# Two-layer graph network on one core: moving the value weights' sums and tile 1's attention in the opening pairs

## The chip, the cores and the metric

The kernel runs on one core of a Trainium2 chip, as a single program. The metric is its time on the device in microseconds; lower is better. A core has five engines that run side by side [...]: TensorE (PE in the profile; its weight loads are listed as PEld), VectorE (DVE), ScalarE (ACT), GpSimd (POOL), and SyncE (SP), which here issues most of the transfers between the device's memory (DRAM) and the on-chip memory (SBUF). Each engine takes its own instructions strictly in order. Results of TensorE land in PSUM banks and are read from there by VectorE or ScalarE. All data are fp32.

## The reference: what is computed

There are 128 graphs of 64 nodes with 768 features. Layer 0 is a graph attention layer with 12 heads of 64 features and a gate, layer 1 an attention layer with 6 heads of 128 features; each is added to its input and normalized:

```python
# layer 0
h = einsum('bnd,ade->bane', x, W)                  # 12 heads
th = tanh(h)
attn = th @ w_src + swap(th @ w_dst)               # one number for each pair of nodes
attn = where(attn >= 0, attn, 0.2 * attn)
attn = softmax(where(~adj, -999.0, attn))
f = elu(attn @ h + b)
gate = sigmoid(x @ H_w.T + H_b)
x = layernorm(x + gate * f + (1 - gate) * x)
# layer 1
q, k, v = x @ Wq + bq, x @ Wk + bk, x @ Wv + bv    # 6 heads
probs = softmax(q @ k.T / sqrt(128) + where(adj, 0, -9e15))
x = layernorm(x + (probs @ v) @ Wf + bf)
```

The layer-1 values v = x @ Wv are computed already in the first phase, pair by pair, as soon as a pair's layer-0 rows are known. They are the only part of layer 1 that the change touches.

## The kernel before

**Tiles and pairs.** The 8192 rows are 64 tiles of 128 rows (two graphs each). Two tiles make a pair p (tiles 2p and 2p+1), so layer 0 has 32 pairs. For a pair, h of all 12 heads and the gate's input are one matrix product: 256 rows by 768, times 768 by 1536. The kernel does it with a scheme that needs 15 block products, called a0 to a14, in place of 18 (class Fifteen). Each takes its own left operand, a block of x or a sum of blocks (made by GpSimd in x_sums, L886), and its own right operand, one of 15 weight blocks. Only 9 of these are loaded as they are; the other weights are sums of them, which VectorE makes at the start (made, L871, 17 steps of 128x1024). The first pair, p = 0, cannot wait for the sums and is computed plainly with the raw blocks (class Plain, 18 products, L987). One product is four matmuls of 128x512.

**Banks.** Products accumulate along five paths (the first number in PRODUCTS), each in a PSUM bank of its own: a0, a3, a6, a9, a11, a13 share one, a8, a10, a12, a14 another, a5 and a7 a third, a2 and a4 a fourth. Between two products of a path the bank is read: its content is added to, or copied into, the tile's buffer hg. This read is the product's way out. The first one into a place is a copy on ScalarE (L968, or L970 with its sign turned), a later one an addition on VectorE (L966). The next product of the path may start only when the way out of the one before has been done.

**Attention of layer 0, for each tile t.** The steps, with the names that the order uses: tanh (function products: tanh on ScalarE, L1019; products with the attention vectors, one half on VectorE, L1020, then the other on GpSimd, L1021), terms (a reduction on VectorE, L1029, and a transpose), send and fetch (the terms to DRAM and back, spread over all partitions), bias (GpSimd, L1052), hx (a copy of the other half of h), logits and leaky (6 ScalarE instructions each, L1072), masked (VectorE: mask L1086 and maximum L1092), exps (12 ScalarE instructions, L1101), probs (transposes on TensorE and copies back), attend (TensorE), feat (VectorE, and an exponential on ScalarE), elu, gated, stats (VectorE), pow (GpSimd), norm (ScalarE), byf (transposes of the result on TensorE, L1113, copied back by ScalarE). Beside them go gbias (GpSimd, L1232), gtanh (ScalarE, L1237 and L1238), resid (GpSimd, L1164), mask (ScalarE turns adj into the mask, L1226), and inputs and plus (loads of x).

**Values.** For each pair the products v1 to v7 (class Job, L349) compute x1 @ Wv with 7 block products in place of 8. They need sums of Wv's four blocks B11, B21, B22, T3: T1 = T3 - B11, T2 = B22 - T1, T4 = B21 - T2, T3 = B22 - T3 (function weight_sums, L295 to L298, one VectorE operation of 128x1152 each), and sums of the rows x1, sum0 to sum3 (L319 to L322). The four blocks are loaded by four transfers of 576 KB on SP's queue (L290).

**The order.** It is written out by hand. EARLY and TURN list the products of all pairs, interleaved; the position of a product in this list is its item. After the product of item i TensorE's instructions are followed, in program order, by the way out of the product of item i - 1, and then by all steps that the plan has put on item i, sorted by their position. The tables NEW_EARLY, OLD_EARLY and SUMS_EARLY (one dict each for p = 0 to 3) give these positions: in OLD_EARLY relative to EARLY_OLD[p] (22 for the first pair) or, for xT and adj, to the start of the next pair; in NEW_EARLY relative to the last of the products that the step needs. Each engine then takes its own instructions in exactly this order. Pair 0 has items 0 to 17, pair 1 items 18 to 32, pair 2 and the values of pair 0 items 33 to 54.

Of the kernel before, what the change touches and what calls it, by code (L numbers as in the profile page):

```python
# [133 lines left out]
EARLY = (  # L134
    "a0 a1 a2 a3 a4 a5 a6 a7 a8 a9 a10 a11 a12 a13 a14 a15 a16 a17".split(),
    "a0 a5 a1 a3 a8 a7 a6 a10 a2 a9 a12 a4 a11 a14 a13".split(),
    "a0 a5 a3 a1 a8 a7 a6 u1 u2 u6 u5 u7 a2 a10 a9 a4 u4 a12 a11 a14 a13 u3".split(),
    "a0 a5 a3 a1 u1 u2 u6 a8 u5 u7 a7 u4 u3 a6 a10 a2 a12 a9 a14 a11 a4 a13 v1 v2".split(),
)
EARLY_OLD = (22, 41, 60)  # L140

# [13 lines left out]
SUMS_LAST = dict(next6=0.4, next9=6.4, next2=0.6, next3=5, next0=15.7, next5=0.1, next8=11.3, own10=1.2, own12=7.8,  # L155
    own13=10.6)
OLD_LAST = dict(probs1=2.1, gtanh1=0.8, resid1=5.8, attend1=5, feat1=5.5, elu1=7, gated1=7.4, stats1=9.3,
    pow1=10.8, norm1=11.6, byf1=13.3, spill1=14.5, logits0=3, leaky0=3.4, masked0=4.4, exps0=5,
    gtanh0=8, resid0=9.7, probs0=8.8, attend0=10.5, feat0=11.8, elu0=12.4, gated0=12.8, stats0=14.5,
    pow0=14.6, norm0=15.6, byf0=16.5, spill0=22.4, sum0=16.5, sum1=17.2, sum2=18.5, sum3=24.4,  # L160
    spillT=24.8, spillV=11, mask=5.1, adj=-1.3, xT=3.4, inputs1=5.9, inputs0=18.5, plus1=13.6,
    plus0=18.9)
OLD_EARLY = [
    dict(probs1=3.1, gtanh1=-2, resid1=-1.5, attend1=3.8, feat1=5, elu1=5.5, gated1=6.1, stats1=7.3,
        pow1=8, norm1=9.8, byf1=10, spill1=13.3, logits0=3.5, leaky0=4.8, masked0=5.2, exps0=7.2,
        gtanh0=3.5, resid0=4.8, probs0=9.8, attend0=10.5, feat0=12, elu0=12.2, gated0=12.3, stats0=14.2,
        pow0=15, norm0=15.7, byf0=17.8, spill0=18.8, sum0=10.2, sum1=18, sum2=19.9, sum3=24.9,
        spillT=21.4, spillV=18.5, mask=7.7, adj=3.9, xT=-5.3, inputs1=6.2, inputs0=17.3, plus1=11.2,
        plus0=18.8),
    dict(probs1=-3.8, gtanh1=1.8, resid1=2.5, attend1=3.3, feat1=4.7, elu1=5.6, gated1=5.8, stats1=6.3,  # L170
        pow1=7, norm1=8, byf1=10, spill1=12.7, logits0=2, leaky0=4, masked0=4.8, exps0=6.8, gtanh0=3.7,
        resid0=6, probs0=8, attend0=9.2, feat0=9.5, elu0=12, gated0=12.4, stats0=13, pow0=14, norm0=16,
        byf0=17, spill0=22, sum0=14.1, sum1=18, sum2=21.5, sum3=24.2, spillT=23, spillV=15.2, mask=5.7,
        adj=4.9, xT=-0.8, inputs1=10.6, inputs0=13.7, plus1=18.5, plus0=14.2),
    dict(probs1=-0.5, gtanh1=1.9, resid1=3.8, attend1=3, feat1=4, elu1=4.2, gated1=5.7, stats1=7.2,
        pow1=8.5, norm1=10.5, byf1=10.8, spill1=12.9, logits0=2.5, leaky0=3.8, masked0=4, exps0=7.3,
        gtanh0=0.7, resid0=4.3, probs0=8.3, attend0=9, feat0=11.5, elu0=12, gated0=12.1, stats0=12.3,
        pow0=13.5, norm0=14, byf0=16.3, spill0=17.5, sum0=16.8, sum1=18.2, sum2=15.7, sum3=20.5,
        spillT=17.8, spillV=8.7, mask=0.8, adj=-2.8, xT=-0.1, inputs1=9.7, inputs0=15.8, plus1=13.2,
        plus0=16.3),  # L180
    dict(probs1=2.6, gtanh1=1.3, resid1=5.5, attend1=3.5, feat1=4.2, elu1=5.5, gated1=5.9, stats1=7.6,
        pow1=8.3, norm1=11, byf1=13.5, spill1=13.8, logits0=2.7, leaky0=3.3, masked0=4.5, exps0=5.9,
        gtanh0=-0.8, resid0=6, probs0=8, attend0=9.8, feat0=10.8, elu0=12, gated0=12.1, stats0=14,
        pow0=15.3, norm0=16, byf0=17.2, spill0=22.6, sum0=14.8, sum1=18.5, sum2=22.5, sum3=20,
        spillT=23.1, spillV=11.6, mask=8.1, adj=5, xT=2.3, inputs1=13.5, inputs0=16.2, plus1=13.6,
        plus0=19.4),
]
NEW_EARLY = [
    dict(tanh1=1.6, terms1=1.8, bias1=1.9, send1=2.5, hx1=7.8, fetch1=4.8, logits1=8.6, leaky1=9.3,
        masked1=12, exps1=12.8, tanh0=1.3, terms0=1.5, bias0=4.1, send0=5.4, hx0=4.7, fetch0=11.5,  # L190
        gbias0=6.8, gbias1=1.2),
    dict(tanh1=1, terms1=2.5, bias1=4.4, send1=4.2, hx1=7.6, fetch1=5, logits1=5.9, leaky1=9.5,
        masked1=10, exps1=10.2, tanh0=1.6, terms0=4, bias0=5.1, send0=7.4, hx0=9.5, fetch0=8.3,
        gbias0=3, gbias1=5),
    dict(tanh1=1.3, terms1=2.3, bias1=5.8, send1=4.7, hx1=9.5, fetch1=5.1, logits1=7.2, leaky1=9.9,
        masked1=10, exps1=11, tanh0=1, terms0=5, bias0=3.4, send0=8.2, hx0=4.3, fetch0=8.5, gbias0=2.7,
        gbias1=2.6),
    dict(tanh1=2, terms1=3.5, bias1=3.5, send1=5, hx1=5.5, fetch1=5.5, logits1=8.3, leaky1=8.4,
        masked1=10.2, exps1=10.5, tanh0=1, terms0=1.9, bias0=6.4, send0=2.3, hx0=9.2, fetch0=3.3,
        gbias0=1.8, gbias1=3.5),  # L200
]
SUMS_EARLY = [
    dict(next6=2.3, next9=3.3, next2=3.7, next3=5, next0=9, next5=6.8, next8=6.5, made0=3, made2=4.1,
        made3=4, made4=4.8, made1=5.1, made5=5.2, made6=6.3, made7=3.7, made9=7, made10=9.1, made8=11.3,
        made11=15, made12=17, made13=19.4, made14=17.2, made15=10, made16=19.6),
    dict(next6=1, next9=0.8, next2=1.2, next3=3.1, next0=5.4, next5=3, next8=0, own10=2.2, own12=5.2,
        own13=2.1),
    dict(next6=4.6, next9=0.1, next2=0.2, next3=1.2, next0=4.4, next5=2.5, next8=2.5, own10=2.4,
        own12=4.1, own13=6.3),
    dict(next6=3.8, next9=0.2, next2=1.2, next3=3.6, next0=7.9, next5=5, next8=8.6, own10=4, own12=4.3,  # L210
        own13=3.1),
]

# [2 lines left out]
def kernel(  # L216
# [33 lines left out]
    V, S, G, T = nc.vector, nc.scalar, nc.gpsimd, nc.tensor  # L250
# [41 lines left out]
    def weight_sums(eng, w):  # L292

        return [
            lambda: eng.tensor_tensor(w[:, T1], w[:, T3], w[:, B11], ALU.subtract),  # L295
            lambda: eng.tensor_tensor(w[:, T2], w[:, B22], w[:, T1], ALU.subtract),
            lambda: eng.tensor_tensor(w[:, T4], w[:, B21], w[:, T2], ALU.subtract),
            lambda: eng.tensor_tensor(w[:, T3], w[:, B22], w[:, T3], ALU.subtract),  # L298
        ]
# [528 lines left out]
    with ExitStack() as ph, ExitStack() as ph_r:  # L828
# [69 lines left out]
        wv_w = wpool.tile([P, 7, HK, HALF], F32, tag="wc", name="wv")  # L898
# [397 lines left out]
        for p in range(NP + 1):  # L1296
# [10 lines left out]
            def at(pos, *acts):  # L1307
                put(new_at[p] + pos, *acts)
# [259 lines left out]
```

## Time and profile before

Three runs took 2805.2, 2807.95 and 2808.09 us; the median is 2807.95. The execution that was profiled took 2808.72 us, of which the span from the first to the last instruction is 2806.5.

| | value |
|---|---|
| median of the runs | 2807.95 us |
| profiled execution | 2808.72 us |
| its span | 2806.5 us |
| TensorE busy | 2783.3 us (99%) |
| VectorE busy | 1842.0 us (66%) |
| ScalarE busy | 1358.1 us (48%) |
| GpSimd busy | 1452.0 us (52%) |
| mean granted clock of TensorE | 0.998 |

A matmul of 128x512 starts every 0.43 us at the full clock, so a product of layer 0 takes 1.72 us. Rows of the timeline give start, duration, engine, line, operation, and in brackets how long the engine stood idle before and what ended that. "y_a", "z_a" are the banks of layer 0's products, "hg" the buffer that the ways out fill, "wa" its weights, "wv" the value weights, "sx" the sums of x, "th" the products with the attention vectors, "dd" the fetched terms, "att" the logits.

### The profile page before, as it was taken

What the parts mean: (1) busy time and instruction counts of PE and PEld (TensorE: products, weight loads), DVE (VectorE), ACT (ScalarE), POOL (GpSimd) and SP (SyncE); (2) the same over time, 40 slices, a digit from 0 to 9 for tenths busy, and PEclk for the clock granted to TensorE, in tenths of its full rate; (3) what the DMA queues carried; (4) which work ended last, traced back from release to release, by engine and by line L of the source; (5) the groups of instructions that cost most, each with busy time, mean ns of one, the idle gap of its engine ahead of it and who ended that gap; (6) DMA issues with size and microseconds to landing.
All of it is one profiled execution on the core that took longest, in us unless ns stands there. A gap on an engine that the chain in (4) does not pass through costs nothing.

```text
span 2806.5 us, 47394 instructions
## 1 busy us (share of the span) xinstructions
PE 2783.3 (99%) x17506; PEld 1934.2 (69%) x17506; DVE 1842.0 (66%) x3199; ACT 1358.1 (48%) x3434; POOL 1452.0 (52%) x1497
## 2 busy tenths in 40 slices
PE   8999999999999999999999999999999999999998
PEld 4555555555555555555568888888888888888887
DVE  6777777778777786777754554555554556554557
ACT  4767676666767667676643221333221333221333
POOL 4555666565665655555454445435345435345435
PEclk9999999999999999999999999999999999999999
DMA  5345444554545445333544212222212222212212
GB/s 196 119 155 160 136 161 135 168 158 138 163 133 182 150 134 162 116 126 115 170 148 158 72 50 80 92 84 80 73 50 80 92 84 80 73 50 80 91 61 83
DMA packets 198039, 325.52 MB, mean 116 GB/s; under 512 B 46897, under 2 KB 125745, under 8 KB 197809
## 3 DMA queue, kind: packets, MB, share of 16 engines
q1 hardware_dynamic: 197520, 322.10, 35.1%
q8 instruction: 140, 2.29, 0.3%
q14 instruction: 91, 0.74, 0.1%
q10 hardware_dynamic: 288, 0.39, 0.0%
HBM read 198.48 MB, written 111.15 MB: 110 GB/s over the span
## 4 chain that ended last, share of the span: by engine, by line
PE 94%; DVE 2%; issue 1%; ACT 0%; POOL 0%; DMA 0%; SPq 0%; ACTq 0%; DVEq 0%; POOLq 0%
PE y_a L950 18%; PE z_a L950 9%; PE z_q L528 9%; PE z_k L528 9%; PE z_o L575 9%; PE y_v L349 8%; PE y_k L528 6%; PE y_q L528 6%; PE y_o L575 6%; PE z_v L349 4%; PE x_v L349 2%; PE av L1134 2%; PE cp L693 2%; PE sp L633 2%; PE pTp L1113 2%; PE x1Tp L1113 1%
## 5 line engine op out<-in xcount | busy, mean ns | idle before, releaser
L950 PE MATMUL y_a<-wa,sx 128*128 128x512 f32 x992 | 468.3, 600 | 3.5 <-ACT hg L970 3.2
L950 PEld LDWEIGHTS y_a<-wa,sx 128*128 128x128 f32 x992 | 182.1, 191 | 197.7 <-issue 160.1
L492 POOL TENSOR_TENSOR so<-ctxT 128x256 f32<-128x256 f32 x224 | 157.9, 729 | 287.8 <-ACT ctxT L720 286.9
L720 ACT ACTIVATE ctxT<-cp,bv_c 128x256 f32<-128x256 f32 x192 | 73.9, 486 | 451.0 <-PE cp L693 451.0
L1164 POOL TENSOR_TENSOR x<-hg,x 128x768 f32<-128x768 f32 x64 | 112.7, 1761 | 211.5 <-ACT hg L1238 211.4
L659 ACT ACTIVATE sc<-sc 128x512 f32<-128x512 f32 x45 | 28.3, 630 | 379.7 <-DVE sc L656 379.7
L528 PE MATMUL z_q<-xs,wa 128*128 128x256 f32 x896 | 211.8, 379 | 0.0
L575 PE MATMUL z_o<-wf,so 128*128 128x256 f32 x896 | 209.2, 381 | 2.4 <-DVE y L588 2.4
L1072 ACT ACTIVATE att<-dd,sd 128x64 f32<-128x64 f32 x768 | 190.7, 336 | 37.9 <-DMA dd<-dstd 37.8
L1101 ACT ACTIVATE prob<-att,mx 128x64 f32<-128x64 f32 x768 | 190.3, 335 | 24.2 <-DVE mx L1092 24.2
L1021 POOL TENSOR_TENSOR th<-th,wsd 128x768 f32<-128x768 f32 x64 | 117.1, 1830 | 162.2 <-DVE th L1020 162.2
L528 PE MATMUL z_k<-xs,wa 128*128 128x256 f32 x840 | 198.4, 379 | 0.0
L401 POOL TENSOR_TENSOR rs_b<-ve_b,minus_half 128x1 f32<-128x1 f32 x64 | 40.9, 640 | 302.2 <-DVE ve_b L399 289.2
L588 DVE TENSOR_TENSOR y<-y,z_o 128x256 f32<-128x256 f32 x320 | 128.6, 419 | 100.3 <-PE z_o L575 100.0
L1086 DVE COPY_PREDICATED_SCALAR att<-nadj,neg 128x768 f32 x64 | 69.2, 1081 | 182.3 <-ACT att L1072 182.3
L575 PEld LDWEIGHTS z_o<-wf,so 128*128 128x128 f32 x896 | 168.7, 190 | 26.9 <-POOL so L492 2.6
L528 PEld LDWEIGHTS z_q<-xs,wa 128*128 128x128 f32 x896 | 169.8, 190 | 23.1
L950 PE MATMUL z_a<-wa,xT 128*128 128x512 f32 x372 | 177.6, 600 | 0.0
L528 PEld LDWEIGHTS z_k<-xs,wa 128*128 128x128 f32 x840 | 159.6, 190 | 21.7
L764 POOL TENSOR_TENSOR y<-y,bf_bc 128x768 f32<-128x768 f32 x64 | 115.0, 1821 | 95.8 <-issue 48.7
L492 POOL TENSOR_TENSOR xs<-r,r 128x512 f32<-128x512 f32 x112 | 146.9, 1330 | 24.4 <-PE z_k L528 13.7
L966 DVE TENSOR_TENSOR hg<-hg,y_a 128x512 f32<-128x512 f32 x217 | 146.7, 676 | 19.4 <-PE y_a L950 15.5
(158 smaller groups left out, 6464.3 us busy)
## 6 DMA issues: line engine op xcount, KB each, us to landing
xT<-in_xT_dram SPq DMA_DIRECT2D x32, 768.0 KB, 7.2
x<-in_x_dram SPq DMA_DIRECT2D x64, 384.0 KB, 3.6
dd<-dstd SPq DMA_DIRECT2D x128, 192.0 KB, 3.5
x1d<-x SPq DMA_DIRECT2D x64, 384.0 KB, 4.9
x1Td<-x1T SPq DMA_DIRECT2D x32, 768.0 KB, 4.8
vd<-v SPq DMA_DIRECT2D x64, 384.0 KB, 3.0
r<-x1Td SPq DMA_DIRECT2D x96, 256.0 KB, 3.4
v<-vd SPq DMA_DIRECT2D x192, 128.0 KB, 3.0
```

Of the source, the lines that this page charges most:

```text
L349: T.matmul(to[:, : self.n], lhsT, rhs, start=kc == 0 and not more, stop=kc == HK - 1, skip_group_check=more,)
L492: G.tensor_tensor(t, self.of(x[0]), self.of(x[2]), x[1])
L528: T.matmul(b[:, half * W2 : (half + 1) * W2], w[:, kc, half * P : (half + 1) * P], x[:, kc, :], start=half == kc == 0 and not more, stop=k ...
L575: T.matmul(b[:, :W2], x[:, kc, :], w[:, kc, :], start=kc == 0 and not more, stop=kc == 1, skip_group_check=more,)
L588: V.tensor_tensor(at, at, self.banks[path][:, :W2], ALU.add if sign > 0 else ALU.subtract)
L764: G.tensor_tensor(y, y, pools["bf"], ALU.add)
L950: T.matmul(b, x[:, kc, :], wa[:, n, kc, :], start=kc == 0 and not more, stop=kc == 1, skip_group_check=more,)
L966: V.tensor_tensor(at, at, b, ALU.add if sign > 0 else ALU.subtract)
L1021: G.tensor_tensor(th[:, 1, :], th[:, 1, :], wsd[:, 1, :], ALU.mult)
L1072: S.activation(att3[:, a], dd3[:, a], AF.Prelu, bias=sd[:, H0 + a : H0 + a + 1], alpha=LEAKY)
L1101: S.activation(prob[:, at * N : (at + 1) * N], att[:, a * N : (a + 1) * N], AF.Exp, bias=mx[:, a : a + 1],)
L1164: G.tensor_tensor(xp, gate_of(t), xp, ALU.mult)
```

## The change

Nothing that is computed changes, only where steps stand in the order. In the first pair:

- logits of tile 1 go from item 18 to item 20 (behind the product a1 of pair 1), leaky from 19 to 20;
- probs of tile 1 go from item 25 to 28, attend from 25 to 29, feat from 27 to 30, elu from 27 to 30, gated from 28 to 31, stats from 29 to 32, pow from 30 to 32, norm from 31 to 34, byf from 32 to 35, spill from 35 to 38, and the first row sum of the values (sum0) from 32 to 35;
- the four transfers of the value weights go from item 16 to item 4, ahead of the transfers of adj and of x (inputs);
- the four sums of the value weights go from items 26, 28, 30, 32 to items 9, 10, 12 and 13;
- made3 goes from item 4 to 3; made16 comes ahead of made13 at item 19; bias of tile 0 goes from item 15 to 13; send 1 comes ahead of tanh 0 at item 12; the mask of pair 1 goes from 25 to 26; the load of xT for pair 3 from 32 to 34.

In pairs 1 to 3 single steps move by one to three items (most inside the same item), and in the product lists a8 goes ahead of a1 in pair 2 and v5 ahead of v1 and v2 among pair 3's.

```diff
@@ EARLY
-    "a0 a5 a3 a1 a8 a7 a6 u1 u2 u6 u5 u7 a2 a10 a9 a4 u4 a12 a11 a14 a13 u3".split(),
-    "a0 a5 a3 a1 u1 u2 u6 a8 u5 u7 a7 u4 u3 a6 a10 a2 a12 a9 a14 a11 a4 a13 v1 v2".split(),
+    "a0 a5 a3 a8 a1 a7 a6 u1 u2 u6 u5 u7 a2 a10 a9 a4 u4 a12 a11 a14 a13 u3".split(),
+    "a0 a5 a3 a1 u5 u1 u2 u6 a8 u7 a7 u4 u3 a6 a10 a2 a12 a9 a14 a11 a4 a13 v1 v2".split(),
@@ OLD_EARLY
-    dict(probs1=3.1, gtanh1=-2, resid1=-1.5, attend1=3.8, feat1=5, elu1=5.5, gated1=6.1, stats1=7.3,
-        pow1=8, norm1=9.8, byf1=10, spill1=13.3, logits0=3.5, leaky0=4.8, masked0=5.2, exps0=7.2,
-        gtanh0=3.5, resid0=4.8, probs0=9.8, attend0=10.5, feat0=12, elu0=12.2, gated0=12.3, stats0=14.2,
-        pow0=15, norm0=15.7, byf0=17.8, spill0=18.8, sum0=10.2, sum1=18, sum2=19.9, sum3=24.9,
-        spillT=21.4, spillV=18.5, mask=7.7, adj=3.9, xT=-5.3, inputs1=6.2, inputs0=17.3, plus1=11.2,
-        plus0=18.8),
+    dict(probs1=6, gtanh1=-2, resid1=-1.5, attend1=7, feat1=8, elu1=8.6, gated1=9, stats1=10, pow1=10.8,
+        norm1=12, byf1=13, spill1=16, logits0=3.5, leaky0=4.8, masked0=5.2, exps0=7.2, gtanh0=3.5,
+        resid0=4.8, probs0=9.8, attend0=10.5, feat0=12, elu0=12.2, gated0=12.3, stats0=14.2, pow0=15,
+        norm0=15.7, byf0=17.8, spill0=18.5, sum0=13.5, sum1=18.3, sum2=19.9, sum3=24.9, spillT=21.4,
+        spillV=18.5, mask=8.7, adj=3.9, xT=-5.3, inputs1=6.2, inputs0=17.3, plus1=11.2, plus0=18.8),
...
@@ NEW_EARLY
-    dict(tanh1=1.6, terms1=1.8, bias1=1.9, send1=2.5, hx1=7.8, fetch1=4.8, logits1=8.6, leaky1=9.3,
-        masked1=12, exps1=12.8, tanh0=1.3, terms0=1.5, bias0=4.1, send0=5.4, hx0=4.7, fetch0=11.5,
-        gbias0=6.8, gbias1=1.2),
+    dict(tanh1=1.3, terms1=1.8, bias1=1.9, send1=2, hx1=7.8, fetch1=4.8, logits1=10.2, leaky1=10.6,
+        masked1=12, exps1=12.8, tanh0=1, terms0=1.5, bias0=2.1, send0=5.4, hx0=4.7, fetch0=11.5,
+        gbias0=6.5, gbias1=1.2),
...
@@ SUMS_EARLY
-        made3=4, made4=4.8, made1=5.1, made5=5.2, made6=6.3, made7=3.7, made9=7, made10=9.1, made8=11.3,
-        made11=15, made12=17, made13=19.4, made14=17.2, made15=10, made16=19.6),
+        made3=3.5, made4=4.8, made1=5.1, made5=5.2, made6=6.3, made7=3.7, made9=7, made10=9.1, made8=11,
+        made11=15, made12=17, made13=19.9, made14=17.2, made15=10, made16=19.6),
...
@@ in the plan of pair 0
                 for block in (B11, B21, T3, B22):
-                    at(16, do(load_block, wv, wv_w, block))
+                    at(4, do(load_block, wv, wv_w, block))
...
-                for pos, act in zip((26, 28, 30, 32), weight_sums(V, wv_w)):
+                for pos, act in zip((9.6, 10.6, 12.6, 13.6), weight_sums(V, wv_w)):
                     at(pos, act)
```

More of the change, by code (lines that the diff above doesn't have):

```diff
@@ L170 @@
[L170 to L174, printed above, removed]
+    dict(probs1=6, gtanh1=-2, resid1=-1.5, attend1=7, feat1=8, elu1=8.6, gated1=9, stats1=10, pow1=10.8,
[3 more added lines that the diff above has]
+        spillV=18.5, mask=8.7, adj=3.9, xT=-5.3, inputs1=6.2, inputs0=17.3, plus1=11.2, plus0=18.8),
@@ L175 @@
+    dict(probs1=-3.8, gtanh1=0.8, resid1=2.5, attend1=3.3, feat1=5, elu1=5.6, gated1=5.8, stats1=6.3,
+        pow1=7, norm1=8, byf1=10, spill1=12.7, logits0=2, leaky0=4, masked0=5.1, exps0=6.8, gtanh0=3.7,
+        resid0=5.7, probs0=8, attend0=9.2, feat0=9.8, elu0=12, gated0=12.4, stats0=13, pow0=14,
+        norm0=16, byf0=17, spill0=22, sum0=14.1, sum1=20, sum2=21.5, sum3=22.2, spillT=23, spillV=15.2,
+        mask=5.7, adj=5.2, xT=1.7, inputs1=10.6, inputs0=13.7, plus1=18.5, plus0=14.2),
     dict(probs1=-0.5, gtanh1=1.9, resid1=3.8, attend1=3, feat1=4, elu1=4.2, gated1=5.7, stats1=7.2,
-        pow1=8.5, norm1=10.5, byf1=10.8, spill1=12.9, logits0=2.5, leaky0=3.8, masked0=4, exps0=7.3,
@@ L177 @@
-        gtanh0=0.7, resid0=4.3, probs0=8.3, attend0=9, feat0=11.5, elu0=12, gated0=12.1, stats0=12.3,
-        pow0=13.5, norm0=14, byf0=16.3, spill0=17.5, sum0=16.8, sum1=18.2, sum2=15.7, sum3=20.5,
-        spillT=17.8, spillV=8.7, mask=0.8, adj=-2.8, xT=-0.1, inputs1=9.7, inputs0=15.8, plus1=13.2,
+        pow1=9, norm1=10.5, byf1=10.8, spill1=12.9, logits0=2.2, leaky0=3.8, masked0=4, exps0=7.3,
+        gtanh0=0.7, resid0=6.3, probs0=8.3, attend0=9.3, feat0=11.5, elu0=12, gated0=12.1, stats0=12.3,
@@ L180 @@
+        pow0=13.5, norm0=14.3, byf0=16.3, spill0=17.5, sum0=16.8, sum1=18.2, sum2=17.7, sum3=20.5,
+        spillT=17.8, spillV=8.7, mask=1.8, adj=-2.3, xT=-0.1, inputs1=6.7, inputs0=15.8, plus1=13.2,
         plus0=16.3),
     dict(probs1=2.6, gtanh1=1.3, resid1=5.5, attend1=3.5, feat1=4.2, elu1=5.5, gated1=5.9, stats1=7.6,
-        pow1=8.3, norm1=11, byf1=13.5, spill1=13.8, logits0=2.7, leaky0=3.3, masked0=4.5, exps0=5.9,
-        gtanh0=-0.8, resid0=6, probs0=8, attend0=9.8, feat0=10.8, elu0=12, gated0=12.1, stats0=14,
@@ L184 @@
-        pow0=15.3, norm0=16, byf0=17.2, spill0=22.6, sum0=14.8, sum1=18.5, sum2=22.5, sum3=20,
-        spillT=23.1, spillV=11.6, mask=8.1, adj=5, xT=2.3, inputs1=13.5, inputs0=16.2, plus1=13.6,
+        pow1=8, norm1=11, byf1=13.5, spill1=13.8, logits0=2.7, leaky0=3.3, masked0=4.5, exps0=5.9,
+        gtanh0=-0.8, resid0=5.7, probs0=8.3, attend0=9.8, feat0=10.8, elu0=12, gated0=12.1, stats0=14.5,
+        pow0=15, norm0=16, byf0=17.2, spill0=22.6, sum0=14.8, sum1=18.5, sum2=22.5, sum3=20,
+        spillT=23.1, spillV=11.3, mask=8.1, adj=6, xT=0.3, inputs1=12.5, inputs0=16.2, plus1=13.6,
@@ L188 @@
 NEW_EARLY = [
-    dict(tanh1=1.6, terms1=1.8, bias1=1.9, send1=2.5, hx1=7.8, fetch1=4.8, logits1=8.6, leaky1=9.3,
-        masked1=12, exps1=12.8, tanh0=1.3, terms0=1.5, bias0=4.1, send0=5.4, hx0=4.7, fetch0=11.5,
-        gbias0=6.8, gbias1=1.2),
-    dict(tanh1=1, terms1=2.5, bias1=4.4, send1=4.2, hx1=7.6, fetch1=5, logits1=5.9, leaky1=9.5,
-        masked1=10, exps1=10.2, tanh0=1.6, terms0=4, bias0=5.1, send0=7.4, hx0=9.5, fetch0=8.3,
+    dict(tanh1=1.3, terms1=1.8, bias1=1.9, send1=2, hx1=7.8, fetch1=4.8, logits1=10.2, leaky1=10.6,
+        masked1=12, exps1=12.8, tanh0=1, terms0=1.5, bias0=2.1, send0=5.4, hx0=4.7, fetch0=11.5,
+        gbias0=6.5, gbias1=1.2),
+    dict(tanh1=1, terms1=2.5, bias1=4.4, send1=4.2, hx1=7.6, fetch1=5.3, logits1=5.9, leaky1=9.5,
+        masked1=10, exps1=10.2, tanh0=1.6, terms0=4, bias0=4.8, send0=7.1, hx0=9.5, fetch0=8.3,
         gbias0=3, gbias1=5),
-    dict(tanh1=1.3, terms1=2.3, bias1=5.8, send1=4.7, hx1=9.5, fetch1=5.1, logits1=7.2, leaky1=9.9,
-        masked1=10, exps1=11, tanh0=1, terms0=5, bias0=3.4, send0=8.2, hx0=4.3, fetch0=8.5, gbias0=2.7,
+    dict(tanh1=1.3, terms1=2.3, bias1=5.8, send1=3.7, hx1=9.5, fetch1=5.1, logits1=7.2, leaky1=9.9,
+        masked1=10, exps1=11, tanh0=1, terms0=5, bias0=3.4, send0=8.2, hx0=3.8, fetch0=8.5, gbias0=2.4,
         gbias1=2.6),
-    dict(tanh1=2, terms1=3.5, bias1=3.5, send1=5, hx1=5.5, fetch1=5.5, logits1=8.3, leaky1=8.4,
+    dict(tanh1=1.7, terms1=3.5, bias1=3.5, send1=5, hx1=5.5, fetch1=5.5, logits1=8.3, leaky1=8.4,
         masked1=10.2, exps1=10.5, tanh0=1, terms0=1.9, bias0=6.4, send0=2.3, hx0=9.2, fetch0=3.3,
-        gbias0=1.8, gbias1=3.5),
+        gbias0=1.8, gbias1=2.5),
 ]
@@ L203 @@
     dict(next6=2.3, next9=3.3, next2=3.7, next3=5, next0=9, next5=6.8, next8=6.5, made0=3, made2=4.1,
-        made3=4, made4=4.8, made1=5.1, made5=5.2, made6=6.3, made7=3.7, made9=7, made10=9.1, made8=11.3,
-        made11=15, made12=17, made13=19.4, made14=17.2, made15=10, made16=19.6),
+        made3=3.5, made4=4.8, made1=5.1, made5=5.2, made6=6.3, made7=3.7, made9=7, made10=9.1, made8=11,
+        made11=15, made12=17, made13=19.9, made14=17.2, made15=10, made16=19.6),
     dict(next6=1, next9=0.8, next2=1.2, next3=3.1, next0=5.4, next5=3, next8=0, own10=2.2, own12=5.2,
         own13=2.1),
-    dict(next6=4.6, next9=0.1, next2=0.2, next3=1.2, next0=4.4, next5=2.5, next8=2.5, own10=2.4,
-        own12=4.1, own13=6.3),
-    dict(next6=3.8, next9=0.2, next2=1.2, next3=3.6, next0=7.9, next5=5, next8=8.6, own10=4, own12=4.3,
+    dict(next6=3.9, next9=0.1, next2=0.2, next3=4.2, next0=4.4, next5=2.5, next8=1.5, own10=2.4,
+        own12=2.1, own13=6.3),
+    dict(next6=3.8, next9=0.7, next2=1.4, next3=3.6, next0=5.9, next5=5, next8=8.6, own10=5, own12=4.3,
         own13=3.1),
```

## The prediction

> **What bounds the kernel now.** I read the page's totals first, then the waits of TensorE by what ended them, then the clock microsecond by microsecond, then the timeline of the first 95 us, where every wait that this change can touch lies.
>
> ```profile
> PE 2783.3 (99%) x17506; PEld 1934.2 (69%) x17506; DVE 1842.0 (66%) x3199; ACT 1358.1 (48%) x3434; POOL 1452.0 (52%) x1497
> ```
>
> TensorE is busy for 2783.3 of 2806.5 us, so all its waits together are 23.2 us, and a schedule that removed every one could gain no more than that and the slow clock behind them. The waits of TensorE over the whole span say which:
>
> ```profile
> PE y_a L950 <- DVE hg L966: 3.3, 2, 3.0
> PE z_o L575 <- DVE y L588: 3.2, 4, 1.7
> PE y_a L950 <- ACT hg L970: 3.2, 1, 3.2
> ...
> PE y_v L349 <- DVE sv_v L320: 0.9, 1, 0.9
> ```
>
> Two single waits, 3.2 us for a ScalarE copy out of PSUM and 3.0 us for a VectorE one, belong to the first two pairs of layer 0; the L575 waits are layer 1's and are not touched. The next view gives, for one microsecond each, TensorE's busy time and instructions, then the granted clock.
>
> ```profile
> 44.00:45.00 1.00, 0.00 (x0) 1.00 0.77 203
> 45.00:46.00 1.00, 0.11 (x1) 0.67 1.07 399
> ...
> 48.00:49.00 1.00, 1.00 (x2) 0.62 1.07 376
> ...
> 69.00:70.00 1.00, 0.00 (x0) 0.62 0.00 0
> ...
> 75.00:76.00 1.00, 1.00 (x3) 0.50 0.70 184
> ```
>
> After each wait the clock is half for a while: until 48.6 and until about 76.2. In the timeline the eight matmuls after the first wait take 4.94 us instead of 8 x 0.43 = 3.43 (1.5 lost), and the two products and six transposes after the second take 7.1 instead of 4.1 (3.0 lost). So the two stalls cost 3.2 + 1.5 + 3.0 + 3.0 = **10.7 us**: that is the prize. The timeline says who is late (start, duration, engine):
>
> ```profile
> 41.31 7.57 DVE L871 TENSOR_TENSOR wa<-wa 128x1024 f32<-128x1024 f32 x5
> 43.82 1.54 ACT L1072 ACTIVATE att<-dd,sd 128x64 f32<-128x64 f32 x6 [4.98 <-DMA dd<-dstd]
> 45.27 0.57 ACT L970 ACTIVATE hg<-y_a 128x512 f32<-128x512 f32 x1
> 51.38 0.68 DVE L966 TENSOR_TENSOR hg<-hg,y_a 128x512 f32<-128x512 f32 x1
> 57.10 1.82 POOL L1021 TENSOR_TENSOR th<-th,wsd 128x768 f32<-128x768 f32 x1 [1.81 <-DVE th L1020]
> 57.54 2.60 DVE L295 TENSOR_TENSOR wv<-wv 128x1152 f32<-128x1152 f32 x1
> 66.23 1.35 DVE L296 TENSOR_TENSOR wv<-wv 128x1152 f32<-128x1152 f32 x1
> 69.36 0.68 DVE L966 TENSOR_TENSOR hg<-hg,y_a 128x512 f32<-128x512 f32 x1
> ```
>
> First stall: ScalarE waits 4.98 us for tile 1's fetched terms, and the copy of product a0 (L970) is queued behind those logits; a3 adds to the same bank and waits. Second: the way out of a12 (69.36) is late because VectorE is busy nearly without a break from 41.3, and a14 waits for it. VectorE is thus late by about five items of the order at 41 us already: it is still making weights (item 19) at 48.9.
>
> **The change, part by part.** *Logits 1 from item 18 to 20, behind the ways out of a0 and a5.* ScalarE then frees a0's bank at about 42, before a3 wants it at 42.55 (a1 starts at 40.83, a product is 1.72). The 3.2 us and its 1.5 of clock are gone. Price: behind a0 and a5, gate tanh 1 waits for gate bias 1 on GpSimd (about 45.1, below), then come its two operations (1.7) and both halves of the logits (3.1): 49.9. Queued behind them is a3's way out, and a6, ready at 47.7, waits for that until about 50.5. This is hidden only if a later thing waits longer, and one does. Without any wait a10 would start at 42.55 + 4 x 1.72 = 49.4 instead of 54.27. It needs two VectorE results: weight 10 (made13, now the last of five) and the way out of a8, which is queued behind tile 1's mask.
>
> *Value weights loaded at 4.* SP issues four DMAs of 576 KB ahead of adj and of the two inputs. Between 7.59 and 12.71 its issues stand 1.28 us apart, the queue being full, about what a 512 KB block takes, so a block costs 1.44. The second xT landed 10.6 us after its issue at 12.71, at 23.3; behind it the third block (T3) lands at 27.6, the fourth at 29.1, adj just behind it instead of at 23.6. ScalarE's mask 0 waits for adj, and the copy of product 10 and tanh 1 wait behind it: tanh 1 goes from 26.2 to about 30.4. TensorE does not wait for that copy (pair 0 has three fresh banks on each side). The weights of layer 0 and both xT stand ahead in the queue and lose nothing. Later the same four DMAs leave SP's queue at 42.2 to 44.5, which frees the sends and fetches there; none of those is waited for once logits 1 has moved.
>
> *Sums of the value weights at 9 to 14.* Four VectorE operations; their rows after 57 us are 2.60, 1.35, 1.35, 1.37 = 6.67 us, and that stretch is relieved. In the new place: made10 ends at 25.4, the first sum waits for T3 until 27.6 (2.2 idle, new). Then sum, made15, sum, made8 = 1.35 + 1.22 + 1.35 + 1.28 = 5.2, and 0.7 for GpSimd's last x sums beside them: 33.4, where tile 1's product with wsd stood at 28.5. That one (0.96) releases GpSimd's (1.8), which releases the reduction: 36.2 instead of 33.72. Tile 0 repeats this and ends its transpose at 43.85 instead of 41.39. Only then come sums 3 and 4: 2 x 1.35, and the five made weights: 5 x 1.22, in all 8.8 us bare.
>
> Beside these GpSimd has the rest of gate bias 1 (1.2), x sum 10 (0.74), residual 1 and gate bias 0 (1.68 each) and two x sums (1.5): 6.8 us. [...] Row: L295 took 2.60 at 57.54, where its sisters took 1.35; GpSimd's product had started at 57.10, and the sum took 1.25 more, the time that product had left. [...] By the row of five made weights the share is smaller: 7.57 instead of 6.1 beside 1.3 + 0.74 us of GpSimd, so 0.72 of it. I take the row: 0.72 x 6.8 = 4.9, **end at 57.5** (before: 48.89); without any contention 52.7.
>
> From there to the end of a8's way out is 3.26 in the rows (48.80 to 52.06: one way out, mask, maximum, way out). So a10 starts at 60.8; 56.0 and 62.8 are the ends.
>
> *Attention of tile 1 three products later, byf 1 into pair 2.* Same operations; they move with a10. From a10 (54.27) to pair 2's a0 (79.51) is 25.24 now; without the stall (3.0), its clock (3.0) and byf 1's transposes (0.65), 18.6. New: slow clock behind a10's stall. Row: 1.5 and 3.0 lost; I take 2.3. [...] And a13 waits about 1.0 for a11's way out, now queued behind features and elu of tile 1. With byf 1's 0.65 put back: 60.8 + 18.6 + 2.3 + 1.0 + 0.65 = 83.35, that is 3.8 later than 79.51. Before v1 at 93.59 TensorE waits 0.6 today, which absorbs as much: **+3.2 us** at v1. VectorE by itself is later by 57.5 - 48.89 - 6.67 = 1.9, less than that, so TensorE's order governs. From 100 on VectorE has waits again (3.45 us for one way out at 104) and no backlog remains.
>
> *Pairs 1 to 3.* Single steps by up to three items, and v5 ahead of v1, which saves the 0.24 that v1 waits at 132. TensorE has under 2 us of waits between 95 and 180. Bounds -1 and +2; I take -0.2.
>
> **Sum:** +3.2 - 0.2 = +3.0. On the profiled execution's own 2808.72 (span 2806.5 and 2.2 around it) 2811.7; the runs' median stands 0.8 lower: **2811.0**. I call a difference under 0.2% (5.6 us) no change, about what a measurement of this kernel can tell.
>
> **Rivals.** With x the end of a8's way out, the shift is x - 54.27 + clock - 5.6.
> *No measurable change (0.55)*, the sum above: x from 56.0 with clock 1.5 to 62.8 with 3.0, shift -2.4 to +5.9, so 2805 to 2814.
> *VectorE's backlog grows (0.33, slower).* Place: the seven operations before a10. Each meets a full GpSimd operation (end 59.5), and the first two sums meet GpSimd's x sums at L295's price (2 x 1.25): x = 65.3, clock 3.0, shift +8.4: 2816.4. It is slower from x = 63 on. For it: GpSimd has work without a break from 39.9 to 50. Against it: the made weights beside x sums took 1.52, not 1.22 + 0.74.
> *The sums fill idle time (0.12, faster).* VectorE waits 7.0 us between 23.4 and 41.3 today (3.75 and 1.93 of it for GpSimd). If the four sums fit there, x stays at 52.1, the clock costs 1.5 and no wait for a11 comes: -2.2 + 1.5 - 6.0 = -6.7: 2801.3. Against it: the sums stand ahead of what ends these waits, and two come after both of them.
>
> **Range and chances.** The likeliest case holds 2805 to 2814. Reaching 2801 below takes in most of the faster case, 2820 above most of the slower: about 8 in 10. Faster 0.12, same 0.55, slower 0.33.
>
> **What would show it.** Right: no wait for L970 near 43; a TensorE wait of several us for an L966 (or for made13) between 49 and 61, then half clock; T3's sum near 27.6; adj landing near 29; tanh 1 near 30; a14's wait gone. Wrong: VectorE's made weights ending before 52, or GpSimd idle beside them; a second stall after 75; or a wait over 2 us in pairs 2 to 4.

## The result and the profile after

The changed kernel takes 2813.59 us (median, 2812.3 to 2814.64), the kernel before, run beside it, 2807.86 (2805.2 to 2810.24). The ratio is 1.0021, with a 95% interval of 1.0014 to 1.0029: 5.7 us slower. The profiled execution took 2812.3 us, its span is 2809.9; before these were 2808.72 and 2806.5. So the two traces stand only 3.4 to 3.6 us apart. The rest of the 5.7 is scatter: before's profiled execution lies 0.9 above the median of its runs, after's 1.3 below. One of the 18 runs of e4 below was a slow one (2912.5 us, at a granted clock of 0.947) and is left out of e4's median. (The line numbers of after are one lower than before's: L949 is L950 of before, and so on.)

The page's totals come first:

```profile
PE 2779.5 (99%) x17506; PEld 1932.7 (69%) x17506; DVE 1845.8 (66%) x3199; ACT 1357.6 (48%) x3434; POOL 1452.3 (52%) x1497
```

TensorE is busy 3.8 us less than before, some 2 us of it because less work falls into half clock (2.4 us lost, below, for 4.5), but it waits 30.4 us in place of 23.2. The waits of TensorE over the whole span say for what (columns: total us, times, longest):

```profile
PE y_a L949 <- DVE hg L965: 10.3, 3, 9.4
PE z_o L574 <- DVE y L587: 3.2, 4, 1.7
PE y_a L949 <- ACT hg L969: 2.5, 1, 2.5
...
PE y_a L949 <- POOL sx L885: 0.7, 1, 0.7
...
PE pTp L1112 <- ACT x1T L1113: 0.6, 1, 0.6
```

Two waits near 3 us, one for ScalarE and one for VectorE, have become a single wait of 9.4 us for VectorE and one of 2.5 for ScalarE, with small new ones behind. The timeline of all engines from 27 to 62 us shows who is late (start, duration, engine, line):

```profile
27.63 1.92 DVE L294 TENSOR_TENSOR wv<-wv 128x1152 f32<-128x1152 f32 x1 [2.08 <-DMA wv<-in_wv_dram]
29.45 0.40 ACT L1225 ACTIVATE nadj<-adj,one 128x128 uint8<-128x128 uint8 x1 [11.80 <-DMA adj<-in_adj_dram]
30.36 0.84 ACT L1018 ACTIVATE th<-hg 128x768 f32<-128x768 f32 x1
...
33.55 0.95 DVE L1019 TENSOR_TENSOR th<-th,wsd 128x768 f32<-128x768 f32 x1
...
43.86 0.21 DVE L1033 STREAM_TRANSPOSE sdT<-sd 128x32 f32<-128x32 f32 x1
44.00 2.52 DVE L296 TENSOR_TENSOR wv<-wv 128x1152 f32<-128x1152 f32 x1
46.44 1.88 DVE L297 TENSOR_TENSOR wv<-wv 128x1152 f32<-128x1152 f32 x1
47.13 2.73 POOL L1163 TENSOR_TENSOR x<-hg,x 128x768 f32<-128x768 f32 x1
48.24 10.30 DVE L870 TENSOR_TENSOR wa<-wa 128x1024 f32<-128x1024 f32 x5
49.81 2.66 POOL L1231 TENSOR_TENSOR hg<-hg,hb_bc 128x768 f32<-128x768 f32 x1
...
50.45 1.98 PE L949 MATMUL y_a<-wa,sx 128*128 128x512 f32 x4 [2.53 <-ACT hg L969]
...
61.02 0.68 DVE L965 TENSOR_TENSOR hg<-hg,y_a 128x512 f32<-128x512 f32 x1
...
61.85 3.75 PE L949 MATMUL y_a<-wa,sx 128*128 128x512 f32 x4 [9.41 <-DVE hg L965]
```

The first sum waits for its block (27.63), and VectorE's steps of the attention stand behind it: tile 1's product comes at 33.55, not at 28.50. The five made weights take 10.30 us where they took 7.57, beside GpSimd operations that themselves take 2.7 us where they took 1.68. They end at 58.54, not at 48.9. The way out of a8 (61.02) stands behind them, and a10 (61.85) waits for it. The clock, one microsecond to a row (TensorE's busy time, matmuls in brackets, granted clock):

```profile
49.00:50.00 1.00, 0.00 (x0) 1.00 0.66 143
...
56.00:57.00 1.00, 0.00 (x0) 0.64 0.00 0
...
63.00:64.00 1.00, 1.00 (x3) 0.50 0.00 0
...
66.00:67.00 1.00, 1.00 (x3) 0.74 0.02 8
```

The wait before a6 leaves the clock full. The one before a10 halves it until 66.5: a10 takes 3.54 us and a2 2.28 in place of 1.72 each, 2.4 lost. Then TensorE's own timeline up to the values:

```profile
79.42 1.98 PE L949 MATMUL y_a<-wa,sx 128*128 128x512 f32 x4 [0.63 <-DVE hg L965]
...
82.96 1.98 PE L949 MATMUL y_a<-wa,sx 128*128 128x512 f32 x4 [0.70 <-POOL sx L885]
...
93.08 0.92 PE L1112 MATMUL pTp<-ident,prob 128*128 128x128 f32 x6 [0.61 <-ACT x1T L1113]
...
98.67 2.20 PE L348 MATMUL y_v<-wv,x1T 128*128 128x384 f32 x6 [0.24 <-ACT x1T L1113]
```

These are a13, pair 2's a0, the transposes of tile 3's probs and v1 (the first of the value products). It starts 5.1 us later than before's (93.59).

### The profile page after: what moved, and what is told of

Same layout as the page of the kernel before. It is cut to its first block, busy times and chain, and to the rows that moved or that the text cites. A ratio compares the mean times of both kernels' runs of the same rounds, so it can differ in the third digit from the quotient of the medians.

```text
span 2809.9 us, 47397 instructions
## 1 busy us (share of the span) xinstructions
PE 2779.5 (99%) x17506; PEld 1932.7 (69%) x17506; DVE 1845.8 (66%) x3199; ACT 1357.6 (48%) x3434; POOL 1452.3 (52%) x1497
## 3 DMA queue, kind: packets, MB, share of 16 engines
q8 instruction: 139, 2.28, 0.3%
## 4 chain that ended last, share of the span: by engine, by line
PE 94%; DVE 1%; ACT 0%; DMA 0%; POOL 0%; issue 0%; SPq 0%; ACTq 0%; DVEq 0%; POOLq 0%
PE y_a L949 18%; PE z_a L949 9%; PE z_q L527 9%; PE z_k L527 9%; PE z_o L574 9%; PE y_v L348 9%; PE y_k L527 6%; PE y_q L527 6%; PE y_o L574 6%; PE z_v L348 4%; PE x_v L348 2%; PE av L1133 2%; PE cp L692 2%; PE sp L632 2%; PE pTp L1112 1%; PE x1Tp L1112 1%
## 5 line engine op out<-in xcount | busy, mean ns | idle before, releaser
L949 PE MATMUL y_a<-wa,sx 128*128 128x512 f32 x992 | 468.4, 600 | 13.6 <-DVE hg L965 10.3
L949 PEld LDWEIGHTS y_a<-wa,sx 128*128 128x128 f32 x992 | 181.5, 190 | 206.9 <-issue 168.0
L949 PE MATMUL z_a<-wa,xT 128*128 128x512 f32 x372 | 177.6, 600 | 0.0
```

The lines of the kernel that those rows point to most:

```text
L949: T.matmul(b, x[:, kc, :], wa[:, n, kc, :], start=kc == 0 and not more, stop=kc == 1, skip_group_check=more,)
```

## The experiments

All are timed against the kernel before on the same chip. One number sums each of them up: the start of the layer-0 product behind v7, at 104.32 us before. What a kernel has lost or won there is within 2.3 us of what it has lost or won in the medians:

| kernel | a10 starts | product behind v7 | against 104.32 | median against before's |
|---|---|---|---|---|
| after | 61.85 | 109.41 | +5.1 | +5.7 |
| e1, sums back | 56.25 | 107.30 | +3.0 | +2.8 |
| e2, adj first | 63.07 | 110.93 | +6.6 | +5.6 |
| e3, logits 1 alone | 55.79 | 106.83 | +2.5 | +2.4 |
| e4, loads and sums alone | 61.17 | 108.90 | +4.6 | +3.7 |
| e5, first pair alone | 61.44 | 109.14 | +4.8 | +6.7 |
| e9, after, GpSimd held back | 57.60 | 107.61 | +3.3 | +3.6 |
| e6, before, sums late | 54.62 | 105.78 | +1.5 | +1.2 |
| e8, after, sums late | 55.56 | 106.51 | +2.2 | +3.3 |
| e10, e9 and sums late | 51.75 | 105.07 | +0.8 | +1.7 |
| e11, sums spread | 52.01 | 101.68 | -2.6 | -0.9 |
| e12, way out first | 51.65 | 100.13 | -4.2 | -1.9 |

**Which part costs it.** e1 is the changed kernel with the sums back in their old place.

```diff
-                for pos, act in zip((9.6, 10.6, 12.6, 13.6), weight_sums(V, wv_w)):
+                for pos, act in zip((26, 28, 30, 32), weight_sums(V, wv_w)):
```

> The changed kernel with the four sums of the value weights back at items 26, 28, 30, 32; their loads stay at item 4. Backlog theory (the sums stand ahead of the made weights on VectorE, and a8's way out is late by them): the five made weights end near 50 instead of 58.5, the way out of a8 near 53.5, a10 starts near 53.5; the sums then stand behind a10 and may cost a second, shorter stall; time 2807 to 2811, that is 3 to 6 us under the changed kernel. Load theory (the loads ahead of adj delay ScalarE, and that is the price): adj still lands near 29, so the time stays at 2812 to 2815.

2810.26 us, ratio 1.0010 [1.0001, 1.0018]. The time is in the range of the first case, but a10 is not where that case put it: the five made weights still take 10.96 us, now from 41.98 to 52.9 (50 was expected); a10 waits 5.82 us and starts at 56.25 (53.5), and the old second stall is back in another place (a13 at 75.97, 2.01). So the sums cost about half of the loss, and the other half comes without them.

e2 keeps everything but lets adj and the inputs be sent ahead of the four blocks.

```diff
-                    at(4, do(load_block, wv, wv_w, block))
+                    at(4.6, do(load_block, wv, wv_w, block))
```

> The changed kernel with adj's load put just ahead of the value weights' loads (these at 4.6 instead of 4). Load theory: adj lands near 23.6 again, tanh 1 on ScalarE runs near 26.2, and the time falls to about 2808. Backlog theory: VectorE reaches tile 1's product with wsd no earlier than 33.5, because it waits for the third block until 27.6 and has two sums and two made weights in front of it, so nothing moves: 2812 to 2815, made weights ending near 58.

```profile
24.53 0.40 ACT L1225 ACTIVATE nadj<-adj,one 128x128 uint8<-128x128 uint8 x1 [6.84 <-DMA adj<-in_adj_dram]
...
29.17 1.63 DVE L294 TENSOR_TENSOR wv<-wv 128x1152 f32<-128x1152 f32 x1 [3.98 <-DMA wv<-in_wv_dram]
```

In this timeline of e2, adj lands in time, and tanh 1 runs at 26.30, but the first sum waits 3.98 us instead of 2.08. 2813.13 us, 1.0020 [1.0012, 1.0028]: nothing is won. The run moves two things at once, since the blocks land 1.5 us later. It does show that an early adj alone frees nothing: tile 1's product on VectorE, which needs tanh 1, still comes only at 34.80, behind the sums in that engine's order. In after too, tanh 1 ends at 31.20 and that product starts at 33.55 without a wait, so the late adj had 2.3 us to spare.

e3 makes only the step that was to remove the first stall, in the kernel before; e4 only the loads and sums.

```diff
# e3, in NEW_EARLY of the first pair of the kernel before
-logits1=8.6, leaky1=9.3
+logits1=10.2, leaky1=10.6
# e4, in the plan of pair 0 of the kernel before
-at(16, do(load_block, ...   zip((26, 28, 30, 32), ...
+at(4, do(load_block, ...    zip((9.6, 10.6, 12.6, 13.6), ...
```

> The kernel before with logits 1 and leaky 1 alone moved to item 20. By the prize reckoning (3.2 of wait and 1.5 of clock go) 2803. Backlog theory: a10 cannot start before VectorE has done a8's way out (52.1 before, about 54 here since GpSimd's residual of tile 1 now runs beside the made weights), a6 waits for ScalarE in between, and the stall near 67 to 70 stays: gain 0 to 3 us, 2805 to 2808.

> The kernel before with only the value weights' loads at item 4 and their sums at 9 to 14; logits 1 and the attention of tile 1 stay where they were. Backlog theory: a8's way out ends near 58 to 61 (logits 1 waits for its terms until about 46 and holds GpSimd's residual back, so the made weights share less than in the changed kernel), a10 starts there, and tile 1's attention, planned three products earlier, makes TensorE wait again for its probabilities: 2811 to 2816. If the changed kernel's price needs both parts, 2807 to 2809.

e3: 2809.89 us, 1.0009 [1.0001, 1.0017], slower by 2.4. e4: 2811.77, 1.0015 [1.0008, 1.0023], by 3.7. Together they make 6.1, about the whole. e4 is as its first case had it. e3 lies outside both of its cases, and the prediction did not foresee a loss either, since the step does remove the first stall. One row of before and then the timeline of e3 say why:

```profile
49.92 1.68 POOL L1164 TENSOR_TENSOR x<-hg,x 128x768 f32<-128x768 f32 x1 [5.64 <-ACT hg L1238]
```

```profile
41.51 10.96 DVE L871 TENSOR_TENSOR wa<-wa 128x1024 f32<-128x1024 f32 x5
...
44.65 2.47 POOL L1164 TENSOR_TENSOR x<-hg,x 128x768 f32<-128x768 f32 x1 [0.16 <-ACT hg L1238]
47.08 2.65 POOL L1232 TENSOR_TENSOR hg<-hg,hb_bc 128x768 f32<-128x768 f32 x1
...
55.79 3.75 PE L950 MATMUL y_a<-wa,sx 128*128 128x512 f32 x4 [5.84 <-DVE hg L966]
```

Before, gate tanh 1 stood on ScalarE behind the waiting logits, so that GpSimd's residual 1 (L1164) started only at 49.92, after 5.64 us of idleness, behind the made weights. With the logits moved, ScalarE is free, residual 1, gate bias 0 and two x sums run beside the made weights, and these take 10.96 us in place of 7.57. The stall that was removed had kept GpSimd out of VectorE's way. Two kernels further down put this to the test, both with the logits in the new place and the sums out of the way: in e8 the made weights take 10.96 us again and a10 starts at 55.56; in e10, where GpSimd is held back, they take 7.59 and a10 starts at 51.75.

e5 takes the steps of pairs 1 to 3 and the product lists back to the kernel before, and leaves the first pair changed.

```diff
# (u1 to u7 are the value products of the pair two before)
# EARLY, and rows 1 to 3 of OLD_EARLY, NEW_EARLY, SUMS_EARLY: as before the change
-    "a0 a5 a3 a8 a1 a7 a6 u1 u2 ...
+    "a0 a5 a3 a1 a8 a7 a6 u1 u2 ...
```

> The change of the first pair alone: the tables and product lists of pairs 1 to 3 are those of the kernel before. If the first pair holds the price, 2812 to 2815, with a10 starting near 61.9 as in the changed kernel. If the small steps of pairs 1 to 3 hold it, about 2808.

2814.24 us, 1.0023 [1.0014, 1.0031]. The whole loss is in the first pair. What the other pairs' steps are worth (+6.7 here against +5.7 for after) is less than these runs can tell.

**Is it GpSimd beside VectorE?** What is called sharing is that operations of the two engines take longer side by side. e9 is the changed kernel with GpSimd's five operations behind x sum 10 put later, beyond the made weights, and with them gate tanh 0 and residual 0, which follow gate bias 0.

```diff
# OLD_EARLY[0], NEW_EARLY[0], SUMS_EARLY[1] of the changed kernel
-resid1=-1.5, gtanh0=3.5, resid0=4.8, gbias0=6.5; next6=1, own12=5.2, own13=2.1
+resid1=4.85, gtanh0=4.9, resid0=4.95, gbias0=9.7; next6=2.65, own12=7.55, own13=4.6
```

> The changed kernel with GpSimd's residual of tile 1, gate bias 0, x sums 12 and 13 and x sum 6 of pair 2 moved behind the terms of tile 3 (item 26), out of the stretch in which VectorE makes the two sums and five weights. Sharing theory [...]: the seven operations take 10.3 to 11 us instead of 14.5, a8's way out ends near 58, a10 starts near 58: 3 to 4 us less, 2809.5 to 2811. Without sharing: seven operations still 14.5 us, 2813 to 2815.

```profile
44.17 2.52 DVE L296 TENSOR_TENSOR wv<-wv 128x1152 f32<-128x1152 f32 x1
46.61 1.88 DVE L297 TENSOR_TENSOR wv<-wv 128x1152 f32<-128x1152 f32 x1
48.42 5.88 DVE L870 TENSOR_TENSOR wa<-wa 128x1024 f32<-128x1024 f32 x5
```

The timeline of e9 shows the same seven operations. The two sums, which still have gate bias 1 and x sum 10 beside them, take the same 2.52 and 1.88; the five made weights, with GpSimd idle, take 5.88 in place of 10.30. a10 starts at 57.60 in place of 61.85. The sharing is thus shown. The time is 2810.89 us (1.0011 [1.0005, 1.0018]), as the case of sharing had it, and a loss of 3.6 where after's is 5.7: of the 4.25 us won at a10, 1.8 are left behind v7, mostly since a4 now waits 1.75 us for a copy on ScalarE.

**Do the sums belong later still?** VectorE's backlog lasts until about 95 us, so in e6 (from before), e8 (from after) and e10 (from e9) the sums stand behind it, close to the products that read them; e8 and e10 also have the loads back at item 16.

```diff
-zip((26, 28, 30, 32), weight_sums          # e6; (9.6, 10.6, 12.6, 13.6) in e8, e10
+zip((39.5, 39.6, 44.5, 42.5), weight_sums
```

> The kernel before with the four sums of the value weights moved later instead of earlier: two to item 39, one each to 42 and 44, just ahead of the value products that use them. Backlog theory: VectorE loses 6.7 us of work between 57 and 76, the wait of a14 (3.0) and the slow clock behind it (3.0) go, the wait of 3.2 for ScalarE stays: 2801 to 2804. If the sums were not what made VectorE late there, 2807 to 2809.

> The changed kernel with the loads back at item 16 and the sums at 39, 39, 42 and 44. Backlog theory: nothing of the value weights stands before a10, but GpSimd's residual and gate bias still run beside the made weights, so these take about 11 us as in the run with logits alone moved (10.96), a10 starts near 55.8, and no second stall comes: 2803 to 2806, that is 8 to 10 under the changed kernel. If the later attention and not the sums is the price, 2811 to 2814.

> Both together: the changed kernel with the loads at item 16, the sums at 39, 39, 42 and 44, and GpSimd's five operations behind item 26. Backlog and sharing theories: five made weights in 7 to 7.6 us, a8's way out near 52, a10 near 52 after a stall of about 2.5, no second stall: 2798 to 2802, under both kernels. If another engine takes over as the bound (ScalarE with logits 1 and gate tanh 0, or GpSimd late with gate bias 0), 2803 to 2808.

They gave 2808.49 (1.0005 [0.9997, 1.0013]), 2810.62 (1.0010 [1.0001, 1.0018]) and 2808.95 us (1.0006 [0.9998, 1.0015]): none beats the kernel before, and all three miss their first case, the hope that late sums would free a10 and a14 for nothing. TensorE's timeline of e6 has the reason:

```profile
69.10 1.98 PE L950 MATMUL y_a<-wa,xT 128*128 128x512 f32 x4 [1.62 <-DVE hg L966]
...
89.86 2.20 PE L349 MATMUL y_v<-wv,x1T 128*128 128x384 f32 x6 [0.24 <-ACT x1T L1114]
...
101.38 3.61 PE L349 MATMUL y_v<-wv,sv_v 128*128 128x384 f32 x6 [2.54 <-DVE wv L298]
```

a14's wait shrinks from 2.98 to 1.62 us and v1 starts 3.7 us earlier than before. So the sums were part of what made VectorE late there, though the time is that of e6's second case. But v7 needs T3, the last sum to be planned (L298), which VectorE now makes behind three row sums and a tile's product and reduction for the attention; it waits 2.54 us and runs at half clock (3.61 in place of 1.93). It starts at 101.38, where it had started at 101.43. e8 and e10 show the same 2.54 us at v7, there at full clock. In e10 ScalarE has taken over as its second case said: a4 waits 2.56 us for a copy on it.

**Each stall moved once more.** e11 is e10 with T3's sum put ahead of two row sums (40.4 in place of 42.5), gate tanh 0 and residual 0 placed so that a4 has no wait, and one x sum so that pair 2's a0 has none. e12 is e11 with two swaps that let a11's way out go ahead of the elu on VectorE.

```diff
# e11, against e10
-zip((39.5, 39.6, 44.5, 42.5), ...   gtanh0=4.9, resid0=4.95   next0=5.4
+zip((39.5, 39.6, 44.5, 40.4), ...   gtanh0=6.9, resid0=6.95   next0=4.9
# e12, against e11
-elu1=8.6, gated1=9,      logits1=5.9 (pair 1)
+elu1=9, gated1=9.05,     logits1=6.9 (pair 1)
```

> The run with both held and late, with its two new waits mended: the fourth sum (T3) goes from 42 to 40, ahead of the row sums, so that v7 does not wait for it (2.5 us there); gate tanh 0 goes behind the ways out of a2 and a9, so that a4 does not wait for it (2.6 us there); x sum 0 of pair 2 goes ahead of x sum 8 (0.7 us). If these waits were what gave the gain back, v7 starts near 97 instead of 102.1 and the time is 2803 to 2806, under the kernel before. If VectorE is the bound up to v7 whatever the order, 2807 to 2809.

> The kernel of e11, with tile 1's elu (tile 1 of the first pair) put behind a11's way out on VectorE, and one half of the next tile's logits put behind the exponential of those features on ScalarE. In e11 a13 waited 2.87 us at 71.20 for a11's way out, queued behind that elu. Theory that a wait moved is a wait gained: a13 starts near 68.4, no half clock behind it, v7 near 96 to 97 (before 101.43), and 2803 to 2806. Theory that VectorE's work up to v7 sets the end of this stretch: a13's wait goes, but v7 still starts at 98 or later behind its last sum, and the time is 2806 to 2808, no measurable difference from the kernel before.

e11: 2807.13 us, 0.9996 [0.9987, 1.0004]. v7 starts without a wait at 98.79, but a13 waits 2.87 us for a11's way out, behind an elu that itself waits 3.45 us for an exponential on ScalarE. e12: 2806.09 us (2805.03 to 2807.54), 0.9992 [0.9984, 1.0001], the lowest of all, though the interval does not exclude that it equals the kernel before. The waits of TensorE over its whole span:

```profile
PE z_o L574 <- DVE y L587: 3.2, 4, 1.7
PE y_a L949 <- POOL sx L885: 2.9, 2, 1.5
PE y_a L949 <- DVE hg L965: 2.4, 2, 2.1
```

a13's wait is gone and v7 stands at 97.24, 4.2 us earlier than before, just past the first expectation's 96 to 97; the time lies where the two expectations meet. GpSimd's x sums now come last (2.9 us in two waits), since they were put behind to spare VectorE. Of the 4.2 us, 2.8 are left at a later product of the values (z_v at 176.76 against 179.60) and 1.9 in the medians; where the rest goes was not followed up.

## Why the prediction was right or wrong

Its place and its order of events held; its size was half of the measured one, +3.0 for +5.7, or 2811.0 for 2813.59. The case called likeliest, no measurable change, ended on its edge: 5.7 us, where 5.6 was set as the bound, and the interval of the ratio (1.0014 to 1.0029) says that the kernel is a little slower and not the same. That the time still lies between 2805 and 2814 is in part luck, since errors of about a microsecond cancelled on the way (below).

- **First stall.** Right in the trace: a3 starts at 42.61 without a wait, and a6 waits instead, until 50.45 (50.5 was forecast). Wrong as a gain: the prediction let this wait vanish at the price of a hidden delay. e3 shows that the step by itself costs 2.4 us. The prediction counted GpSimd's residual 1 and gate bias 0 among what lies beside the made weights, but booked them under the sums of the value weights; they belong to the logits, whose wait had held them back (e3, and e8 against e10).
- **Loads.** First block's sum at 27.63 (27.6), adj read at 29.45 (29), tanh 1 at 30.36 (30.4), VectorE's product for tile 1 at 33.55 (33.4), tile 0's transpose at 43.86 done 0.2 later (43.85). The adj part of this chain is slack, as the rows of after and e2 show.
- **Made weights and sums.** Forecast to end at 57.5, ended at 58.54. The seven operations took 14.54 us, not 8.8 + 4.9 = 13.7. GpSimd's own work beside them was 7.6 us and not 6.8, since a third x sum (0.74) fell in, and the share was larger than 0.72. e9 measures it: 4.42 us more for five operations beside 1.68 + 1.68 + 3 x 0.74 = 5.58 of GpSimd, 0.79. The 59.5 of the second rival is 43.85 + 8.8 + 6.8, with all of GpSimd's time added. The measured 58.54 lies halfway between 57.5 and 59.5, but with the 7.6 us that really stood beside the seven, adding all of it gives 43.85 + 8.8 + 7.6 = 60.3 and the row's 0.72 gives 58.1: the row was nearer. The reading of L295 was a little off too: the product that it met had 1.38 us left, and the sum took 1.25 more.
- **a10 and the clock.** a10 at 61.85 (60.8), half clock behind it worth 2.4 (2.3), a13's wait 0.63 (1.0). Right.
- **From a10 to v1.** This is the term that was too small: +3.2 forecast, +5.1 measured. At pair 2's a0 the balance was still right, +4.1 (82.96 + 0.65 for the moved transposes, against 79.51) for +3.8, but by luck: the later a10 (1.05) and a wait of 0.70 for an x sum on GpSimd, which no step had named, were made up for by the rest, which took 17.4 us (21.11 - 2.4 - 0.63 - 0.70) and not 18.6: with a product between the transposes and attend, attend had no wait for the transposed copy (0.24 each before) and ran more quickly (0.9 us in place of 1.2). Then the step "before v1 TensorE waits 0.6 today, which absorbs as much" failed. The wait before v1 stayed, because what v1 needs moved with everything else, and TensorE's way from a0 to v1 became 1.0 us longer (15.71 for 14.08, with 0.65 of the difference for the transposes that moved), most of it a new wait of 0.6 before the transposes of tile 3's probs. So 4.1 + 1.0 = 5.1, where the prediction had 3.8 - 0.6 = 3.2.
- **Pairs 1 to 3.** Forecast -0.2. e5 puts them at -1.0 by the medians and at +0.3 by the product behind v7, within what the runs can tell.
- **Profile and median.** Between the two profiled spans there are 3.4 us, near the +3.0 of the sum; between the medians 5.7. The shift at v1 (5.1) agrees with the medians. In the trace of after 0.8 of it is gone at a later product of the values (180.12 against 175.87) and 0.9 more at the end of the span. Whether that is more than the scatter of single executions is open.
- **Rivals.** That the sums fill idle time is excluded: the first waits for its block, and the last two run after both idle stretches. That VectorE's backlog grows is what happened in kind: e9 shows the sharing, at 0.79 of GpSimd's time where that rival assumed all of it. Its point of decision (a8's way out ending at 63) was not reached, it ended at 61.70; without the 0.7 and the 0.6 us of the two unnamed waits the loss would have stayed clear of the bound.

## What to carry to other kernels

Where several engines are a few microseconds late in turn, removing the wait that is seen releases work that the wait had held back; ask, before counting the gain, beside which operations that work will run, as GpSimd's residual did here beside the made weights (2.47 us in e3 for 1.68 before). Take a stall's gain to where the next result of the late engine is needed (here a10, a14, a13, v7 in turn), and take slack as an asset only if what ends it does not move along. The start of one fixed product behind the changed stretch, read from a single trace, had the sign of the median's change in all twelve kernels and lay within 2.3 us of it; for the four kernels nearest to the one before (e6, e10, e11, e12) the runs themselves do not establish a change.

## What the runs showed of the hardware

In after, the made weights and GpSimd's operations both took longer side by side. Together 5.88 + 5.58 = 11.46 us of work took 10.3 us, so the two engines won 1.2 us over one after the other. In the single rows of after, two made weights of 2.7 us meet two GpSimd additions of 2.7, then three of 1.6 to 1.7 meet three x sums of 1.7. Away from these meetings a made weight takes 1.22 us (the median of the 17 in before), such an addition 1.68 and an x sum 0.74 (before, at 49.92 and 53.19). So a weight and a GpSimd operation took about as long as one after the other, less 0.2 to 0.3 us (2.7 for 1.22 + 1.68 = 2.90, 1.7 for 1.22 + 0.74 = 1.96). Not every meeting cost that: before's residual 1 took 1.68 us beside VectorE's mask and maximum, which took 1.08 and 0.95, and take 1.06 and 0.95 in e9 with GpSimd idle. What to count is therefore which operations meet, more than a share of the time.

Whether a short wait halves the clock was not decided by its length alone. In e10 and e12 the same product waits almost equally long at the same place, 2.07 us until 51.75 and 2.06 until 51.65. The clock of e10, a microsecond to a row, and then that of e12:

```profile
51.00:52.00 1.00, 0.25 (x1) 1.00 0.39 74
52.00:53.00 1.00, 1.00 (x3) 0.88 0.61 132
53.00:54.00 1.00, 1.00 (x2) 0.50 0.23 51
```

```profile
51.00:52.00 1.00, 0.35 (x1) 1.00 0.50 49
52.00:53.00 1.00, 1.00 (x3) 1.00 0.68 153
53.00:54.00 1.00, 1.00 (x4) 1.00 0.20 30
```

In e10 the clock falls a microsecond after TensorE is back at work and stays half until 56.2; in e12 it stays full from 44 to 100 us. The wait of 2.53 us before a6 in after cost no clock either, while before's 3.18 and 2.98 cost 1.5 and 3.0 us.

A row of 0.88 was full clock for 0.76 of its microsecond and half clock for 0.24, so e10's clock fell at 52.76. Worked out like this, the half clock lasts 3.42 us in e10 (52.76 to 56.18), 3.42 and 6.82 in before (45.34 to 48.76 and 69.24 to 76.06), 10.24 in after (56.28 to 66.52) and 13.66 in e2 (52.30 to 65.96): once, twice, three and four times the shortest. What sets these lengths, and what decides behind which short wait the clock falls, was not shown. A price for the clock behind a short wait is therefore a range, from nothing to 3.0 us behind the waits of 2 to 3.2 us here.
